# An attention kernel on one Trainium2 core: a new order for the second attention's list, with two scalings moved into it

## The chip, the cores and the metric

The kernel runs on one core of a Trainium2 chip. All data are float32. The metric is the device time of one execution in microseconds; lower is better. The profile uses short names for the engines: PE is TensorE (PEld its weight loads), DVE is VectorE, ACT is ScalarE, POOL is GpSimd, SP is SyncE, which here issues the stores.

## The reference

`x` and `ctx` have 32 batches of 256 tokens with 256 features. The computation, cut to what matters:

```python
# 1. multi-head attention of x over ctx; only batch 0 of its result is used
x = x + attention16(x, ctx, Wq, Wk, Wv)[0]
# 2. first attention of this block, over the layer-normed ctx
nx = layernorm(ctx, norm1_w, norm1_b)
nf = layernorm(x, norm2_w, norm2_b)
att = softmax(nf @ nx.T / 16) @ nx
h = gelu(att @ fc1_w.T + fc1_b)          # 4 hidden units per token
c = h @ fc2_w.T + fc2_b
# 3. second attention: c over itself, after a layernorm
nc = layernorm(c, norm3_w, norm3_b)
s = softmax(nc @ nc.T / 16) @ nc
out = nf + gamma2 * (c + gamma1 * s)
```

The 4 hidden units make everything in part 3 a function of few numbers per token: `c` is 5 numbers (4 and a one) times a fixed matrix, and `nc` is 6 numbers times a fixed matrix. So the kernel computes the second attention on rows of 5 or 6 numbers, and one last product with a fixed matrix `w_out` gives the 256 output features.

## The kernel before, in words

Batches are numbered 0 to 31. Four batches form a group `g` (0 to 7), two form a pair `p` (0 to 15; group `g` holds pairs 2g and 2g+1). All of x stays on the chip in `x_all`, and the output is built up in it.

**First part.** `first_step(s)` for s = 0 to 31 does a step of the first attention for batch s (scores, softmax, transposes), and pieces of layer norms for later batches. `first_step(32)` to `first_step(34)` finish it. In between, steps 20 to 31 already do pieces of the second attention for the first groups.

**norm2_w.** `x_all` holds x normalised but not yet multiplied by norm2_w. `scale_skip(n)` (line 770) does that for batch n: one multiplication on POOL of 128 x 512 numbers by a row that is broadcast. The output of batch n can be added only after it. The list `scaled_at` says at which step of the first part the scalings 0, 1, 2 and so on are issued. Within `first_step` they come after the work that POOL has for later batches.

**The second attention.** It is one list of words, `order`, read from left to right. Each word issues one piece, and each engine does its pieces in the order in which they were issued. The words, for group g or pair p:

- `pre6`, `gelu6`, `m3`, `vg3`, `vgv3`, `var3`, `r3`, `t_k3`: hidden units and layer norm of groups 6 and 7. `n7` copies the last first-attention result to `n_all`. `pre` runs on POOL (lines 993, 995), `gelu` on ACT (996, with a load of its function table), `m` on POOL (1010), `vg` on DVE (1024), `vgv` on POOL (1030), `var` on DVE (1039), `r` on POOL (1046 to 1051, ending in a second product of line 1010, `w_k`), `t_k` on DVE (1055). `t_k2` is the last of these for groups 4 and 5.
- `turn_u g`, `uT g`: four transposes on PE, then a copy out of PSUM (1078). They give the operands of the scores.
- `q p@bank`: first scores of pair p on PE (line 445), `max p` their maxima on DVE (1196), into column NK of `t_sl`.
- `turn_t g`, `tT g`: two transposes and a copy (1088) that bring those maxima into the operand of the second scores.
- `k p@bank`: second scores, less the maxima, and `exp p` on ACT (1209).
- `sums g` (line 357), `col g` (368), `turn_a g` (1117), `a g` (1122, 1123): weighted sums, a copy, transposes, and the division into `v_sl`.
- `turn_v g`, `vT g`: transposes and copy (1088) of `v_sl`.
- `o p@bank`: the output product of pair p on PE, and `add p` on DVE (1214), which adds it to `x_all` and is followed by the store of the two batches from SP's queue (1215, 512 KB).
- `scale n`: `scale_skip(n)` on POOL.

A copy word with `.v` behind it runs on DVE, otherwise on ACT.

**Pair products.** `q`, `k` and `o` are products with 32 rows of weights. Pair p uses partitions 0 to 63 when p is even and 64 to 127 when it is odd. Words joined by `+` are issued interleaved, row group by row group:

```python
for t in range(NC):
    for p, lhs, rhs, dst in pairs:
        for i in range(2):
            r = SL * (p % 2 * 2 + i)
            nc.tensor.matmul(dst[i][:, t, :], lhs[r : r + SL, t * P : (t + 1) * P], rhs[r : r + SL, :], ...)
```

So a product of one pair is 8 matmul records in the profile (float32 gives two each), and of two pairs 16.

**Buffers.** In PSUM, `s0` and `s1` are one buffer of two banks each, `et` has two banks that a pair takes together, and `tp` has two banks that all transposes and `sums` take in turn. A piece waits until the previous user of its banks was read. The copies `ut`, `tt`, `vt` and `col` have three buffers each.

## Time and profile before

| | us |
|---|---|
| median of 3 runs | 230.23 |
| lowest, highest | 229.31, 233.49 |
| profiled execution, own time | 233.63 |
| its span from the first to the last instruction | 231.9 |
| PE busy | 214.7 (93%) |
| POOL busy | 174.8 (75%) |
| DVE busy | 169.8 (73%) |
| ACT busy | 146.8 (63%) |
| mean granted TensorE clock | 0.969 |
| bytes moved | 33.81 MB, 146 GB/s in the mean |

The list takes the last quarter of the span: its first transposes start on PE at 176.59 us, PE's last product starts at 223.09, and the last addition on DVE ends at 227.0. A span row of a window gives busy time, with the number of instructions in brackets, for PE, PEld, DVE, ACT and POOL in that order, and then the granted clock, the share of DMA time and GB/s. Matmuls overlap, so PE's busy time doesn't tell how full it is; the number of instructions in a window helps.

### The profile page before, as it was taken

The numbers are of one execution on the slowest core, as the hardware profiler recorded it, in microseconds if no ns is written. First come the engines' busy times: TensorE is split into PE (matmuls) and PEld (weight loads), VectorE is DVE, ScalarE is ACT, GpSimd is POOL, SyncE is SP. The second block draws the span as 40 slices with busy tenths as digits, with TensorE's granted clock in tenths as the row PEclk, the third lists the DMA queues.
The fourth block names the chain that finished last, engine by engine and source line by source line (L and its number), as shares of the span: only waits on it lengthen the run. The fifth ranks groups of instructions, "written<-read, shape, count | busy, mean of one in ns | idle before, by whom it ended". The sixth has DMA issues, their size and how long they took to land.

```text
span 231.9 us, 4950 instructions
## 1 busy us (share of the span) xinstructions
PE 214.7 (93%) x1797; PEld 155.8 (67%) x1797; DVE 169.8 (73%) x409; ACT 146.8 (63%) x299; POOL 174.8 (75%) x276
## 2 busy tenths in 40 slices
PE   7999898898999989999999999989989999999960
PEld 6766556576787768697897887866665666566540
DVE  1797989899988748667686686766384866588791
ACT  2544978698988285966789967456846753444410
POOL 6057598576989999999979999995189999993000
PEclk9999999999999999999999999999999995699996
DMA  6789997999959964180720000000000130444477
GB/s 212 271 310 371 394 383 148 194 256 236 207 104 335 275 117 170 34 151 2 133 51 1 3 0 0 3 4 4 4 0 3 51 133 0 181 184 181 185 281 264
DMA packets 18038, 33.81 MB, mean 146 GB/s; under 512 B 1175, under 2 KB 2142, under 8 KB 18014
## 3 DMA queue, kind: packets, MB, share of 16 engines
q1 hardware_dynamic: 12974, 24.33, 29.3%
q0 software_dynamic: 3696, 7.34, 18.1%
q10 hardware_dynamic: 1344, 1.84, 2.3%
q8 instruction: 14, 0.23, 0.4%
q14 instruction: 10, 0.08, 0.1%
HBM read 17.73 MB, written 8.39 MB: 113 GB/s over the span
## 4 chain that ended last, share of the span: by engine, by line
PE 53%; POOL 23%; DVE 14%; ACT 5%; issue 2%; DVEq 0%; POOLq 0%; ACTq 0%
PE sc L779 13%; POOL x_all L770 5%; PE k L445 4%; PE pt_x L202 4%; PE o L445 3%; PE pt_c L202 3%; POOL cq L307 3%; DVE st L211 3%; PE pt_e L202 3%; PE pu L357 3%; POOL rs_b L227 3%; PE sc L445 2%; POOL rs_x L227 2%; PE ph L357 2%; PE pf L357 2%
## 5 line engine op out<-in xcount | busy, mean ns | idle before, releaser
L779 PE MATMUL sc<-nxT,nfT 128*128 128x256 f32 x256 | 62.4, 386 | 0.7 <-ACT nfT L761 0.7
L779 PEld LDWEIGHTS sc<-nxT,nfT 128*128 128x128 f32 x256 | 45.7, 190 | 12.1 <-issue 5.3
L770 POOL TENSOR_TENSOR x_all<-x_all,w_bc 128x512 f32<-128x512 f32 x32 | 39.8, 1273 | 0.0
L792 ACT ACTIVATE e<-sc,nm 128x256 f32<-128x256 f32 x64 | 26.9, 473 | 19.0 <-DVE nm L789 18.8
L789 DVE TENSOR_REDUCE nm<-sc 128x2 f32<-128x512 f32 x32 | 22.0, 688 | 22.9 <-PE sc L779 11.1
L761 ACT ACTIVATE nfT<-pt_x,bq,wq 128x256 f32<-128x256 f32 x64 | 33.3, 583 | 1.6 <-PE pt_x L202 1.5
L1214 DVE TENSOR_TENSOR x_all<-o,x_all 128x512 f32<-128x512 f32 (+1 forms) x22 | 19.4, 927 | 8.0 <-PE o L445 8.0
L211 DVE BATCH_NORM_STATS2 st<-x_all 128x6 f32<-128x256 f32 x64 | 23.2, 411 | 0.6 <-DMA x_all<-att 0.5
L1209 ACT ACTIVATE eT<-k 128x1024 f32<-128x1024 f32 (+1 forms) x16 | 14.2, 916 | 13.2 <-PE k L445 10.5
L202 PE MATMUL pt_x<-ident,x_all 128*128 128x128 f32 x132 | 20.8, 280 | 1.5 <-POOL x_all L329 1.3
L202 PE MATMUL pt_c<-ident,cq 128*128 128x128 f32 x132 | 19.7, 276 | 1.5 <-ACT nfT L761 1.0
L202 PE MATMUL pt_e<-ident,e 128*128 128x128 f32 x128 | 19.5, 275 | 1.3 <-ACT eTq L801 0.7
L211 DVE BATCH_NORM_STATS2 st<-cq 128x6 f32<-128x256 f32 x56 | 20.6, 412 | 0.0
L307 POOL TENSOR_SCALAR cq<-cq,rs_b,nmr_b 128x256 f32<-128x256 f32 x32 | 19.4, 680 | 0.0
L202 PEld LDWEIGHTS pt_e<-ident,e 128*128 128x128 f32 x128 | 15.4, 141 | 5.0 <-ACT e L792 1.6
L202 PEld LDWEIGHTS pt_x<-ident,x_all 128*128 128x128 f32 x132 | 15.5, 143 | 4.7 <-POOL x_all L329 2.4
L801 ACT COPY eTq<-pt_e 128x512 f32<-128x512 f32 x32 | 18.4, 588 | 0.3 <-PE pt_e L202 0.3
L345 DVE COPY nxT<-pt_c 128x512 f32<-128x512 f32 x23 | 15.6, 677 | 2.3 <-PE pt_c L202 2.3
L202 PEld LDWEIGHTS pt_c<-ident,cq 128*128 128x128 f32 x132 | 15.0, 141 | 3.1 <-ACT nfT L761 1.9
L331 ACT ACTIVATE x_all<-x_all,nmr_b,rs_b 128x256 f32<-128x256 f32 x16 | 9.8, 618 | 10.9 <-POOL nmr_b L236 10.9
L445 PE MATMUL o<-w_out,vt 32*128 32x256 f32 x128 | 15.0, 448 | 0.6 <-ACT vt L1088 0.5
L445 PE MATMUL k<-tt,ut 32*128 32x256 f32 x112 | 15.3, 441 | 0.1
(222 smaller groups left out, 443.8 us busy)
## 6 DMA issues: line engine op xcount, KB each, us to landing
out_dram<-x_all SPq DMA_DIRECT2D x16, 512.0 KB
x_all<-att POOLq DMA_DIRECT2D x7, 1024.0 KB, 9.3
cq<-in_ctx_dram SPq DMA_DIRECT2D x6, 1024.0 KB
x_all<-in_x_dram SPq DMA_DIRECT2D x4, 1024.0 KB
x_all<-in_x_dram SPq DMA_DIRECT2D x1, 2048.0 KB
x_all<-in_x_dram SPq DMA_DIRECT2D x1, 1792.0 KB
cq<-in_ctx_dram ACTq DMA_DIRECT2D x1, 1024.0 KB
cq<-in_ctx_dram SPq DMA_DIRECT2D x1, 768.0 KB
```

The source lines that it names most:

```text
L202: nc.tensor.transpose(pt[:, dc, t * P : (t + 1) * P], src[:, t, dc * P : (dc + 1) * P], ident)
L211: nc.vector.bn_stats(st[:, t, :], src[:, t, :])
L307: nc.gpsimd.tensor_scalar(row, row, rs[:, i + t, :], nmr[:, i + t, :], ALU.mult, ALU.add)
L357: nc.tensor.matmul(pg[SL * b : SL * (b + 1), 0, :], weights(kc, b), moving[:, b, kc, :], start=(kc == 0), stop=(kc == NC - 1),)
L445: nc.tensor.matmul(dst[i][:, t, :], lhs[r : r + SL, t * P : (t + 1) * P], rhs[r : r + SL, :], start=True, stop=True,)
L761: nc.scalar.activation(nfT_of[n][:, dc, :], px[:, dc, :], AF.Identity, bias=bq[:, dc : dc + 1], scale=wq2[:, dc : dc + 1],)
L770: nc.gpsimd.tensor_mul(x_all[:, n], x_all[:, n], w2_bc.unsqueeze(1).to_broadcast([P, NC, D]))
L779: nc.tensor.matmul(sc[:, qt, :], nfT[:, dc, qt * P : (qt + 1) * P], nxT[:, dc, :], start=(dc == 0), stop=(dc == NC - 1),)
L789: nc.vector.tensor_reduce(nm, sc, AX.X, ALU.max, negate=True)
L792: nc.scalar.activation(e[:, qt, :], sc[:, qt, :], AF.Exp, bias=nm[:, qt : qt + 1])
L801: nc.scalar.copy(eT_of[q][:, b], turned(e_of.pop(n), "et", f"e_{n}"))
L1214: nc.vector.tensor_add(xs, po, xs)
```

## The change

The list is replaced by another order of the same pieces. The pieces keep their engines but for some copies: `vT0`, `vT1`, `vT2`, `uT6`, `tT7`, `col1` and `col4` run on DVE in the new list and on ACT in the old one; `tT4`, `uT5`, `vT3`, `vT4`, `col5` and `col6` the other way round. The products are joined in other pairs and use other banks, group 7 is finished ahead of group 6 (`turn_u7` before `turn_u6`), and `pre6` follows `scale11` where it followed `scale15`. The scalings of batches 10 and 11 are no longer issued in `first_step(32)` but are words of the list.

```diff
-    scaled_at = [25, 26, 26, 27, 27, 28, 29, 29, 31, 31, 32, 32]
+    scaled_at = [25, 26, 26, 27, 27, 28, 29, 29, 31, 31]
...
     order = """
-    turn_v0 scale12 q7@s1+q6@et t_k2 vT0 scale13 turn_t2 max7 sums1 tT2 scale14 max6
-    k5@s0+k4@s1 col1 turn_n7 exp5 scale15 turn_u5 n7 o1@et uT5.v exp4 pre6 turn_t3 add1
-    scale16 q11@s1+o0@s0 tT3 gelu6 sums2 max11 scale17 turn_u4 col2 add0 m3 turn_a1 uT4
-    k7@s1+q10@et scale18 a1 vg3 turn_a2 q8@s0 max10 exp7 vgv3 scale19 turn_v1 var3
-    q9@s1+k6@et a2 vT1 max8 r3 turn_v2 exp6 turn_t5 max9 o2@s0 tT5 vT2 o3@et+k10@s1 add2
-    turn_t4 exp10 add3 sums3 k11@s1+o4@s0 tT4.v col3 scale20 t_k3 turn_a3 exp11 add4
-    turn_u6 scale21 o5@et uT6 a3 scale22 q12@s0+k9@s1 add5 turn_v3 exp9 scale23 max12
-    sums5 k8@s1+q13@et col5.v scale24 vT3.v turn_u7 exp8 max13 scale25 o7@s0 uT7 turn_t6
-    scale26 add7 q15@et+o6@s1 tT6 turn_a5 scale27 max15 sums4 a5 scale28 q14@s0+k13@et
-    col4 add6 turn_a4 exp13 scale29 turn_v5 max14 k12@s1 vT5 a4 scale30 o11@s0+o10@et
-    exp12 turn_t7 add11 scale31 sums6 tT7 add10 k15@s1+k14@s0 col6.v turn_v4 exp15
-    turn_a6 vT4.v a6 exp14 o8@et+o9@s1 sums7 add9 turn_v6 col7 add8 vT6 turn_a7
-    o13@s1+o12@s0 a7 turn_v7 add13 vT7 o14@et add12 o15@s1 add14 add15
+    turn_t2 scale10 q7@s1+q6@et t_k2 tT2 turn_n7 max7 scale11 k5@s0 n7 turn_v0 exp5
+    turn_u4 pre6 vT0.v max6 uT4 scale12 o0@s1+o1@s0 gelu6 turn_t3 add0 sums1 tT3 m3
+    k4@et+q9@s1 col1.v add1 scale13 turn_a1 exp4 turn_u5 max9 scale14 q8@s0 uT5 vg3
+    q11@s1+k6@et a1 vgv3 var3 turn_v1 max8 r3 exp6 sums2 vT1.v k7@s0+q10@et col2 max11
+    turn_a2 exp7 turn_t4 max10 o3@s1 tT4 a2 o2@et+k9@s0 add3 scale15 turn_v2 exp9 sums3
+    vT2.v t_k3 scale16 o5@s0+k8@s1 col3 add2 turn_a3 exp8 scale17 turn_u7 add5 o4@et uT7
+    scale18 a3 q15@s0+q14@s1 add4 scale19 turn_t5 max14 turn_u6 tT5 turn_v3 scale20
+    uT6.v vT3 k10@et+k11@s1 max15 scale21 sums4 exp11 turn_t7 exp10 scale22
+    q12@s1+q13@s0 tT7.v col4.v turn_a4 max12 scale23 sums5 a4 k15@et+o6@s1 col5 scale24
+    max13 turn_a5 exp15 turn_v4 scale25 add6 k14@s0 vT4 a5 scale26 o8@s1+o7@et exp14
+    turn_t6 add8 scale27 sums7 tT6 add7 turn_v5 col7 scale28 o9@s1+k12@s0 vT5 k13@et
+    add9 exp12 scale29 turn_a7 exp13 o10@s0+o11@s1 scale30 a7 sums6 add10 scale31
+    turn_v7 col6 add11 vT7 turn_a6 o15@s0+o14@et a6 turn_v6 add15 vT6 o12@s1 add14
+    o13@s0 add12 add13
     """
```

## The prediction

> **What bounds the kernel now.** First the engines' totals and the clock row of the page.

> ```profile
> PE 214.7 (93%) x1797; PEld 155.8 (67%) x1797; DVE 169.8 (73%) x409; ACT 146.8 (63%) x299; POOL 174.8 (75%) x276
> PEclk9999999999999999999999999999999995699996
> ```

> PE is busy nearly everywhere, and two slices near 200 us show a granted clock far below full. The change touches only what follows 176.59 us, where PE takes up the list. So the second view is that stretch in windows of 3.41 us (columns: busy time and instructions of PE, PEld, DVE, ACT, POOL, then granted clock, DMA share, GB/s).

> ```profile
> 183.57:186.98 3.41, 3.41 (x47) 1.84 (x40) 2.84 (x5) 2.88 (x5) 3.33 (x5) 1.00 0.41 154
> 186.98:190.40 3.42, 3.27 (x22) 1.85 (x26) 2.04 (x6) 1.84 (x3) 3.42 (x5) 1.00 0.42 158
> 190.40:193.81 3.41, 3.41 (x22) 2.22 (x20) 2.45 (x3) 1.84 (x4) 3.33 (x3) 0.50 0.00 0
> 193.81:197.21 3.40, 3.40 (x22) 2.17 (x18) 2.11 (x3) 0.40 (x1) 3.24 (x4) 0.50 0.00 0
> 197.21:200.62 3.41, 3.41 (x30) 1.82 (x32) 1.36 (x3) 1.00 (x2) 3.41 (x4) 0.50 0.82 308
> 200.62:204.03 3.41, 3.41 (x40) 2.25 (x32) 2.65 (x5) 1.61 (x3) 3.41 (x4) 1.00 0.19 73
> ```

> From 190.40 to 200.62 PE runs at half clock. The window ahead of it began only 22 matmuls; the full-clock windows of the list up to 221 otherwise begin 40 or more, and after one with 30 the clock comes back. Why so few? The chain of waits and the timeline say:

> ```profile
> 179.30 4.92 POOL x_all L770 x4
> 184.56 0.29 POOL pre L995
> 184.85 2.46 POOL x_all L770 x2
> 187.31 0.99 POOL w_m L1010
> 188.33 0.57 DVE vg L1024
> 188.90 0.61 DVE t_sl L1196
> 189.55 1.17 PE k L445 x3
> ```
> ```profile
> 188.33 0.57 DVE L1024 TENSOR_REDUCE vg<-w_m 128x80 f32<-128x400 f32 x1 [1.72 <-POOL w_m L1010]
> 188.81 1.28 DVE L1196 TENSOR_REDUCE t_sl<-q 128x2 f32<-128x512 f32 x2
> ```

> POOL works off six scalings (176.79 to 184.2) before `pre6`, so `gelu6` and `m3` come late. DVE stands 1.72 us before `vg3`, with `max10` queued behind it. `max10` must empty the two `et` banks before `k6`, so `q9` runs alone from 188.70 and `k6` from 189.55: two half-filled products after `q8`, itself a single one.

> [...] the trace gives 1.07 us for a product of two pairs (16 matmuls, even and odd pair) and 1.06 for a single one (8). [...]

> **The change part by part.** *PE's work.* Both lists hold 38 pair products in 23 issues, 15 double and 8 single: 15 x 1.07 + 8 x 1.06 = 24.5. Then 7 `sums` x 1.00, 21 turns x 0.37, 4 `turn_u` x 0.59 and `turn_n7` 0.28, in all 41.9, less 0.5 where the last two singles overlap (both lists): 41.4. Nothing is added or removed.

> *What before takes for it.* 176.59 to 224.72 is 48.13. At half clock it did: the rest of `q9`/`k6` 0.75, `turn_v2` and `turn_t5` 0.65, `o2` 1.06, `o3+k10` 1.07, `turn_t4` 0.37, `sums3` 1.00, most of `k11+o4` 0.87 = 5.77 at full-clock prices, in 10.22: 4.45 lost to the clock. That leaves 43.7, so 2.3 are waits: about 1 around `q9`/`k6`, 0.5 before `o14`, the rest small.

> *The scalings.* Two of 1.235 leave POOL's queue after `w_k2` (ends 176.8) and enter the list. POOL then does `scale10`, `scale11` to 179.3, and `turn_n7` has moved up, so `n7` and its reciprocal on DVE end at 179.7 behind `max7`. `pre6` ends at 180.4 (before 184.85), `gelu6` at 182.57 after its 1.28 table load (before 185.15), `m3` 183.6 (188.3), `w_k3` about 192.0 (196.1). Then 17 scalings x 1.235 end at 213.0 (before 12, at 210.90). `add15`, which needs the last two, can start at 216.5, and `add8` needs `scale17`, done 195.7, at 208.3: cost nothing, 3.5 us of cover.

> *The list laid out* by hand at full clock, each engine in its own order, with 0.1 from PE to its reader, max or add 1.14 (1.2 as two halves), exp 0.98 (1.05 as halves), copies 0.34 to 0.6. PE issue, then the last thing that it needs: `k5` 178.31 (`tT2` 177.97); `o0+o1` 180.50 (`exp5` leaves s0 180.45, a wait of 0.17); `k4+q9` 182.94 (`add0` 182.87); `turn_a1` 184.01 (`col1` 183.44); `q8` 184.97 (`add1` 184.58); `q11+k6` 186.03 (`uT5` 185.92); `turn_v1` 187.10 (`a1` 186.6, queued behind `vg3`, whose `m3` is 2 us early); `k7+q10` 188.47 (`exp6` 188.28); `o2+k9` 191.34 (`tT4` 191.03); `o5+k8` 193.78 (`exp9` 193.53); `q15+q14` 196.87 (`uT7` 196.55); `k10+k11` 199.40 (`max14` 199.35, wait 0.13); `q12+q13` 201.84 (`exp11` 201.59); `k15+o6` 204.28 (`max12` 204.2); `k14` 206.09 (`max13` 205.8); `o8+o7` 207.15 (`add6` 206.87); `o9+k12` 209.96 (`add8` 209.5); `k13` 211.03 (`add7` 210.7); `o10+o11` 212.46 (`add9` 212.33); `turn_a6` 215.04 (`col6` 215.0, 0.14); `o15+o14` 215.42 (`vT7`); `o12` 217.38 (`vT6`, 0.52), `o13` to 219.0. Waits about 1.0 where before had 2.3.

> *The end.* After `a6` four adds of two batches remain in both lists, 4.7 us of DVE in one piece: 216.57 to 221.2. Before, its last add ended at 227.0, 222.55 without the 4.45. The last store follows as before: adds every 1.15 us or more, bytes 1.0 us after an add, 1.4 us a store in a row; this puts the last byte 3.2 after the last add (before 230.1 - 227.0 = 3.1).

> *Sum.* The layout gains 222.55 - 221.2 = 1.35. Many margins are under 0.1; bounds on what they give back are 0 and 2.4 (twenty places by 0.12), and I take 0.35. Own time of the profiled execution 233.63 (span 231.9 and 1.7 around it), less 4.45 that the clock took, less 1.0: 228.2. The median of 230.23 and the lowest, 229.31, stand near 233.63 - 4.45 = 229.2, so most runs shown lose little or nothing to the clock, and against them only the 1.0 remains.

> **The rivals.** *Forecast*, 0.53: full clock in the whole list, one microsecond less waiting; 228.2, its own range 227.2 to 229.0. *The wait moves to DVE*, 0.25: DVE has some 17.8 us of work in the layout's 19.4 from `add0` at 181.65 to the end of `max15` at 201.1, and no long pause in it; if a dozen of the thin margins are overrun by 0.1, the gain is gone: 229.4. For it: margins of 0.05 to 0.1 at `o0+o1`, `k4+q9`, `k10+k11`. Against it: between 200.95 and 221.06 before shows PE steps back to back with only 0.4 lost behind such margins. *Slower: the half clock falls into the new list*, 0.17. Its place is between `sums3` and `sums4`, 6.7 us without a `sums`, with `o4` alone among turns: about 32 matmuls in a window, near the 30 at which the clock came back. Three windows cost 4.45: 232.7; one, 1.7: 229.9. It decides from the point where a window begins some 22 to 28, that is where PE stands 0.5 us more there. *More than forecast*, 0.05: the earlier `w_k3` and fewer single products side by side save 1.5 more, 226.7. That the edit does nothing is no rival: POOL's order does change.

> **How the numbers follow.** Likeliest 228.2. From 226.7 to 231.4 I leave out the worst half of the third rival and part of the last. Faster by over 2% means under 225.6, which needs 3.6 us of waits removed where 2.3 exist: 0.05, kept for a comparison with an execution that lost 4.45. Slower by over 2%, above 234.8, needs the half clock and the lost margins together: 0.03. Within 2%, about what a measurement of this kernel can tell from no change: 0.92.

> **What would show it.** Right: `pre6` at about 180, DVE's idle time before `vg3` under 0.3, a granted clock of 1.00 in every window from 176.6, PE's last product near 219, the last add near 221, a span near 226.5. Wrong: PE waiting on `max`, `add` or `exp` in many places of the list by more than 1.5 us in all (rival two); any 0.50 window before 219 (rival three); POOL still scaling when `add15` waits.

## The result, and the profile after

The new list takes 227.96 us in the median of 11 runs (226.96 to 229.17); the kernel before, run beside it, 229.31 in the median of 11. The ratio is 0.9941, with a 95% interval from 0.9922 to 0.9961: the change gains about 1.35 us, 0.6%, which is within 2%. A later comparison, below, gave 0.9912 (0.9892 to 0.9932) for the same kernel, some 2.0 us. Three of those 11 executions of before took some 233.5 us, like the profiled one, in which the clock fell to half within the list; the ratios leave such executions out. The profiled execution of the new kernel took 228.16, its span 226.4. Forecast were 228.2 and "near 226.5".

First the page: PE's busy time and the clock row. PE's 214.7 us have become 208.1 with the same 1797 instructions, and no slice inside the list is under full clock. The 6 at the end is the time after the last product.

```profile
PE 208.1 (92%) x1797; PEld 152.6 (67%) x1797; DVE 169.8 (75%) x406; ACT 146.6 (65%) x301; POOL 175.3 (77%) x276
PEclk9999999999999999999999999999999999999996
```

The same stretch in windows (busy time and instructions of PE, PEld, DVE, ACT, POOL, granted clock, DMA share, GB/s). Before, one such window held 22 matmuls (a count takes in one that runs across the border) and three at half clock, 0.50, followed it. None of these five holds fewer than 38, and DVE is busy for 3.0 to 3.35 of 3.4 us in all five.

```profile
182.60:186.00 3.40, 3.40 (x43) 2.26 (x44) 2.98 (x4) 3.25 (x7) 2.84 (x3) 1.00 0.41 154
186.00:189.40 3.40, 3.40 (x48) 1.96 (x48) 3.25 (x8) 1.60 (x4) 2.62 (x4) 1.00 0.41 154
189.40:192.80 3.40, 3.40 (x45) 2.35 (x38) 3.32 (x6) 1.49 (x4) 3.24 (x4) 1.00 0.02 5
192.80:196.20 3.40, 3.40 (x42) 2.12 (x43) 3.35 (x6) 2.32 (x4) 3.40 (x4) 1.00 0.41 154
196.20:199.60 3.40, 3.32 (x38) 2.31 (x36) 3.19 (x7) 1.21 (x4) 3.40 (x4) 1.00 0.91 343
```

The timeline shows why. On POOL, `pre6` now comes at 180.64 and `m3` at 183.16; they came at 184.56 and 187.31. POOL had to wait 1.00 for `gelu6` and has idle time again. The rest of the scalings is one block of 17 after `w_k3`.

```profile
180.64 0.29 POOL L995 TENSOR_TENSOR pre<-pre,fc1b_all 128x64 f32<-128x64 f32 x1
183.16 1.03 POOL L1010 TENSOR_TENSOR w_m<-v_sl,gram_m 128x400 f32<-128x400 f32 x1 [1.00 <-ACT v_sl L996]
191.47 1.34 POOL L1010 TENSOR_TENSOR w_k<-u_sl,gram_k 128x576 f32<-128x576 f32 x1
192.76 20.98 POOL L770 TENSOR_TENSOR x_all<-x_all,w_bc 128x512 f32<-128x512 f32 x17
```

On DVE, `vg3` follows a maximum without a gap (before: 1.72 us of standing), and the adds of the last four pairs are one piece (five instructions, as one pair is added in halves).

```profile
185.21 1.22 DVE L1196 TENSOR_REDUCE t_sl<-q 128x4 f32<-128x1024 f32 x1
186.34 0.56 DVE L1024 TENSOR_REDUCE vg<-w_m 128x80 f32<-128x400 f32 x1
216.74 4.68 DVE L1214 TENSOR_TENSOR x_all<-o,x_all 128x1024 f32<-128x1024 f32 x5 [0.52 <-PE o L445]
```

PE's timeline names one wait in the whole list, in front of the last two products. It is the 0.52 for `vT6` that the layout gave for `o12`. Shorter stops are not named there: the window from 196.20 above lacks 0.08 us of PE.

```profile
217.52 1.63 PE L445 MATMUL o<-w_out,vt 32*128 32x256 f32 x16 [0.52 <-ACT vt L1088]
```

One difference is not the list's: its first transposes start at 177.02 here and at 176.59 in the profile before, though nothing ahead of them was changed. Over the profiles of all kernels below this start lies between 176.27 and 178.03. So lists are compared by their own length, from that start to the end of the span. Before took 231.9 - 176.59 = 55.31, or 50.86 without the 4.45 that the prediction gives to the half clock. After takes 226.4 - 177.02 = 49.38. The list gained 1.48 us beside the clock; 1.0 was forecast.

### The profile page after: what moved, and what is told of

It is laid out like the page before. It is cut to its first block, busy times and chain, and to the rows that moved or that the text cites. A ratio compares the mean times of both kernels' runs of the same rounds, so it can differ in the third digit from the quotient of the medians.

```text
span 226.4 us, 4951 instructions
## 1 busy us (share of the span) xinstructions
PE 208.1 (92%) x1797; PEld 152.6 (67%) x1797; DVE 169.8 (75%) x406; ACT 146.6 (65%) x301; POOL 175.3 (77%) x276
## 3 DMA queue, kind: packets, MB, share of 16 engines
q10 hardware_dynamic: 1344, 1.84, 2.5%
## 4 chain that ended last, share of the span: by engine, by line
PE 45%; POOL 22%; DVE 14%; DMA 8%; ACT 5%; issue 3%; DVEq 1%; ACTq 0%; SPq 0%; POOLq 0%
PE sc L779 8%; POOL cq L307 6%; PE o L445 4%; DMA x_all<-att 4%; POOL rs_b L227 4%; PE k L445 4%; DVE st L211 4%; PE pu L357 4%; POOL x_all L329 3%; PE sc L445 2%; PE q L445 2%; DVE nm L789 2%; DMA wk_nat<-in_L_xattn_Wk_dram 2%; DMA fc_nat<-in_L_xattn_fc_w_dram 2%; POOL rs_x L227 2%
## 5 line engine op out<-in xcount | busy, mean ns | idle before, releaser
L770 POOL TENSOR_TENSOR x_all<-x_all,w_bc 128x512 f32<-128x512 f32 x32 | 39.8, 1278 | 0.0
L1214 DVE TENSOR_TENSOR x_all<-o,x_all 128x1024 f32<-128x1024 f32 (+1 forms) x20 | 19.3, 1005 | 2.9 <-PE o L445 2.4
L1209 ACT ACTIVATE eT<-k 128x512 f32<-128x512 f32 (+1 forms) x19 | 14.3, 798 | 9.1 <-PE k L445 7.8
L307 POOL TENSOR_SCALAR cq<-cq,rs_b,nmr_b 128x256 f32<-128x256 f32 x32 | 19.4, 679 | 0.0
L445 PE MATMUL o<-w_out,vt 32*128 32x256 f32 x128 | 13.3, 400 | 0.6 <-ACT vt L1088 0.5
L445 PE MATMUL k<-tt,ut 32*128 32x256 f32 x112 | 13.6, 397 | 0.0
```

Of the source, the lines that this page charges most:

```text
L307: nc.gpsimd.tensor_scalar(row, row, rs[:, i + t, :], nmr[:, i + t, :], ALU.mult, ALU.add)
L770: nc.gpsimd.tensor_mul(x_all[:, n], x_all[:, n], w2_bc.unsqueeze(1).to_broadcast([P, NC, D]))
L1214: nc.vector.tensor_add(xs, po, xs)
```

## The experiments

**Theory.** The gain comes from POOL's order alone: with fewer scalings ahead of `pre6` and `m3`, group 6 and 7's layer norm comes in time, DVE's queue doesn't stand and PE's products stay joined. The order of the products themselves matters little. **Rivals:** it comes from the new order of the products; or any edit that takes `vg3` out of `max10`'s way would do; or the list was and is bound by DVE.

### POOL's order alone, in the old list

```diff
-... n7 o1@et uT5.v exp4 pre6 ...             (scale12 to scale15 ahead of pre6, 16 to 19 up to r3)
+... n7 o1@et uT5.v exp4 pre6 scale12 ... m3 scale13 scale14 ... r3 scale15 scale16 scale17 scale18 scale19 ...
```

> The old list with POOL's order of the new one alone: scale12 to scale19 are put behind pre6, m3 and r3, so that pre6 follows scale11. Every other engine keeps the old order. Theory (late POOL work costs before its time): m3 ends near 185.8 instead of 188.3, DVE's idle time before vg3 falls from 1.72 to under 0.3 us, q9 and k6 run as one double product, and 0.8 to 1.0 us go: ratio to before near 0.996, and no window of half clock in the profile. Rival (the order of PE's, DVE's and ACT's pieces makes the gain): under 0.3 us, ratio 0.999 to 1.001.

Measured: 227.88 (22 runs) against 229.33, ratio 0.9951 (0.9936 to 0.9967). That interval overlaps with that of the new kernel (0.9922 to 0.9961), though not with that of its later comparison (0.9892 to 0.9932, on another chip). In the timeline of POOL `m3` comes at 185.69 where it was 187.31, although the list starts 0.85 later here (177.44), and on DVE `vg3` has no idle time ahead of it:

```profile
182.75 0.29 POOL L995 TENSOR_TENSOR pre<-pre,fc1b_all 128x64 f32<-128x64 f32 x1
185.69 1.03 POOL L1010 TENSOR_TENSOR w_m<-v_sl,gram_m 128x400 f32<-128x400 f32 x1 [1.42 <-ACT v_sl L996]
```
```profile
187.37 0.56 DVE L1024 TENSOR_REDUCE vg<-w_m 128x80 f32<-128x400 f32 x1
187.99 1.29 DVE L1196 TENSOR_REDUCE t_sl<-q 128x2 f32<-128x512 f32 x2
```

`q9` and `k6` run joined from 189.64:

```profile
189.64 0.48 PE L445 MATMUL q<-ut 32*128 32x256 f32 x2
189.65 0.48 PE L445 MATMUL k<-tt,ut 32*128 32x256 f32 x2
```

The list has 226.9 - 177.44 = 49.46 us: 1.40 of the 1.48 is had with eight words moved and every product left where it was. By the times the share is smaller: in this same comparison the third experiment below, which has the whole new order, took 227.48 at a ratio of 0.993, so that POOL's order gives 1.1 of 1.6 us by the two ratios. It has between two thirds and nearly all of the gain; that it is the whole of it is not shown. The thinnest window of this list that was read holds 33 matmuls, and its clock is full.

### POOL late again, in the new list

```diff
-... turn_u4 pre6 vT0.v ... (scale12 to scale15 spread behind it)
+... turn_u4 scale12 scale13 scale14 scale15 pre6 vT0.v ...
```

> The new list with scale12 to scale15 put back ahead of pre6, where the old list had them; nothing else. Theory (POOL's lateness is the cost): pre6 ends near 185.3 instead of 180.9, gelu6 holds up tT3 and exp4 on ACT and vg3 holds up a1 and max8 on DVE, PE waits 2 to 3 us more than in the new list: 230 to 231 us, and a window of half clock near 190 in some executions. Rival (margins of the new list absorb it): under 0.5 us more, 228 to 228.5.

Measured: 232.25 (231.46 and 231.48, 233.01 and 233.04), ratio 1.0142 (1.0104 to 1.0179): slower than before, and by more than was expected. The timelines of ACT and PE give the way that it takes. `gelu6` waits for `pre6` with the copies `tT3` and `uT5` queued behind it on ACT, so `turn_a1` and `q11` wait on PE:

```profile
184.87 0.26 ACT L996 ACTIVATE v_sl<-pre 128x64 f32<-128x64 f32 x1 [2.46 <-POOL pre L995]
```
```profile
185.44 0.44 PE L1117 MATMUL pt_a<-ident,col_u 128*128 128x128 f32 x2 [1.09 <-ACT tt L1088]
188.32 0.53 PE L445 MATMUL q<-ut 32*128 32x256 f32 x2 [0.94 <-ACT ut L1078]
190.70 1.71 PE L357 MATMUL pu<-eT,u_sl 128*32 128x256 f32 x16
```

The last of these lines is a `sums`, 1.07 at full clock: the clock fell behind the two waits. The window in which it was low, and the one in front of it (the fall itself lies at 188.63 and the rise at 192.05, and in the 3.41 us up to the fall PE began only 18 matmuls):

```profile
185.60:189.00 3.40, 2.46 (x22) 1.83 (x25) 2.68 (x6) 2.65 (x4) 2.27 (x4) 0.95 0.41 154
189.00:192.40 3.40, 3.40 (x34) 1.32 (x27) 1.56 (x2) 1.08 (x2) 3.24 (x3) 0.55 0.03 5
```

The list has 229.7 - 176.62 = 53.08, 3.70 more than after. Half of the 3.42 us at half clock, an estimate of 1.7 us, was lost to the clock; with the waits of 1.09 + 0.94 that makes 3.73. The two pairs of times here, 1.55 apart, look like one such stretch and two; no profile shows the second. So POOL's order carries the gain in the new list too, and what it guards is worth more than the gain: the new list has less slack against a late `pre6` than the old one, in which the clock fell in only some executions. The profile shows the fall in one of these four executions; for the other three it is read from their times and mean clocks (0.985, 0.973 and 0.973).

### The two scalings back in the first attention's last step

```diff
-    scaled_at = [25, 26, 26, 27, 27, 28, 29, 29, 31, 31]
+    scaled_at = [25, 26, 26, 27, 27, 28, 29, 29, 31, 31, 32, 32]
...
-    turn_t2 scale10 q7@s1+q6@et t_k2 tT2 turn_n7 max7 scale11 k5@s0 ...
+    turn_t2 q7@s1+q6@et t_k2 tT2 turn_n7 max7 k5@s0 ...
```

> The new list with the two scalings of batches 10 and 11 issued in the first attention's last step again, so only this part of the change is undone. POOL does them behind the same w_k2 and ahead of the same pre6 in both: theory expects no difference, 0.998 to 1.002 against the new kernel. Rival (their place counts): slower by 0.5 us or more.

Measured: 227.48 (11 runs), ratio 0.993 (0.9909 to 0.9951), list 225.6 - 176.27 = 49.33. No difference from the new kernel. The scalings of batches 10 and 11 come to POOL behind `w_k2` either way; that they are words of the list now costs and gains nothing.

### The old list with `max10` ahead of `vg3`

Is it enough to take the waiting instruction out of `max10`'s way?

```diff
-... a1 vg3 turn_a2 q8@s0 max10 exp7 ...
+... a1 turn_a2 q8@s0 max10 vg3 exp7 ...
```

> The old list with max10 ahead of vg3 on DVE, everything else as before; POOL stays as late as it was. Theory (k6 waits because max10 is queued behind vg3, which waits for POOL): max10 starts near 187, k6 runs joined with q9 at 188.7, vg3 starts at the same 188.3 as before; 0.7 to 0.9 us gained, ratio near 0.9965, and the half clock gone. Rival (the late w_k3 holds PE up elsewhere, so the wait only moves): under 0.3 us, ratio 0.999 or more.

Measured: 228.83 (14 runs), ratio 0.9988 (0.997 to 1.0006): no gain that can be told from none. `q9` and `k6` were joined, at 188.59, as the prediction's reading of before wants it. But the wait moved on. The timelines of DVE, PE and POOL:

```profile
188.14 0.56 DVE L1024 TENSOR_REDUCE vg<-w_m 128x80 f32<-128x400 f32 x1
189.60 0.24 DVE L1039 TENSOR_REDUCE var<-vgv 128x16 f32<-128x80 f32 x1 [0.90 <-POOL vgv L1030]
```
```profile
190.33 0.41 PE L1063 MATMUL pt_v<-ident,v_sl 128*128 128x128 f32 x2 [0.60 <-DVE v_sl L1123]
191.37 1.13 PE L445 MATMUL o<-w_out,vt 32*128 32x256 f32 x12 [0.41 <-DVE t_sl L1196]
```

```profile
187.99 1.27 POOL L770 TENSOR_TENSOR x_all<-x_all,w_bc 128x512 f32<-128x512 f32 x1
189.22 0.34 POOL L1030 TENSOR_TENSOR vgv<-vg,v_sl 128x80 f32<-128x80 f32 x1
```

DVE now stands at `var3`, for a `vgv3` that POOL begins only at 189.22, behind a scaling. `a2` is queued behind it, `turn_v2` waits for `a2`, and so on. The list has 50.81 us, the 50.86 of before. The separated products were the place where the lateness showed, and not its cause.

### Is DVE the bound?

Two experiments on the new list. One puts ten sums of 128 x 256 numbers, which nothing reads, behind nine maxima and adds and one copy. The other takes three copies from DVE and gives them to ACT.

```diff
+... col1.v wait1 ... max9 wait1 ... add3 wait1 ...     (ten in all)
+        nc.vector.tensor_reduce(idle_dve, w2_bc, AX.X, ALU.add)
```

> The new list with ten extra sums on DVE (128x256 from SBUF, some 0.35 us each, read by nobody) behind col1, max9, max8, max11, max10, add3, add2, add5, add4 and max14: 3.5 us more DVE work between 182.6 and 199.6, where DVE has about 0.9 us idle in the new kernel's trace. Theory (PE and DVE are both nearly full there, so the list stands on thin margins): 2.2 to 2.8 us slower than the new kernel, near 230.3, perhaps with half clock on top. Rival (DVE has room, PE alone sets the pace): under 1 us, 228.5 or less.

Measured: 230.51 (5 runs), ratio 1.0058 (1.0019 to 1.0097). A sum takes 0.41 us in the trace and delays the next instruction by 0.33, so 3.3 were added; the list grew from 49.38 to 229.7 - 178.03 = 51.67, by 2.3. By the ratios it is more, 2.7 us against the new kernel's 0.9941 and 3.3 against its 0.9912. Most of what DVE is given comes out at the end:

```profile
187.40:190.80 3.40, 3.30 (x46) 1.75 (x48) 3.25 (x9) 1.30 (x3) 1.96 (x4) 1.00 0.41 154
190.80:194.20 3.40, 3.35 (x38) 2.21 (x33) 3.37 (x8) 1.45 (x3) 3.24 (x3) 1.00 0.02 5
```

DVE is as busy as in the windows of after, and PE lacks 0.10 and 0.05 us in these two (3.30 and 3.35 of 3.40).

```diff
-... vT1.v ... vT2.v ... uT6.v ...
+... vT1 ... vT2 ... uT6 ...
```

> The new list with the copies vT1, vT2 and uT6 on ACT instead of DVE: 1.28 us less DVE work between 188 and 200, onto an ACT that is idle there by a third or more. Theory (DVE and PE are both full there, so what slows DVE by 3.3 us costs nearly all of it, but PE's own steps stand behind it): at most PE's wait of 0.24 us near 198.7 goes, 0 to 0.3 us gained. Rival (DVE alone sets the pace): 0.8 to 1.2 us gained.

Measured: 228.14 (6 runs), ratio 0.9943 (0.9922 to 0.9964), list 226.1 - 176.59 = 49.51. Nothing is gained. The new kernel itself, beside it, took 227.38, and so did, within 0.01, the kernel below that has the same copies on ACT, so the 0.8 us between them is not put down to the copies. DVE has no room for 3.3 us more, but 1.3 us less on it doesn't shorten anything. What fits is that PE has no gap there that could close: its timeline in this run names only the 0.5 us ahead of `o12`.

### What lets the clock fall

The prediction's third rival put the half clock into the new list, between `sums3` and `sums4`, from about 22 to 28 matmuls in a window. Both experiments lengthen that place, behind `o4`: one with 12 transposes of the identity, the other with 6 products of one row group, two records each. The 1.7 us that the prediction and both expectations give to one window is an estimate: half of 3.41, a third of the 10.24 us at half clock in the kernel before. With POOL late one such stretch came alone, of 3.42 us.

```diff
-... o4@et uT7 ...
+... o4@et fill6 uT7 ...
+        for i in range(12):                               # first experiment
+            nc.tensor.transpose(pf[:, 0, P * (i % 2) : P * (i % 2 + 1)], ident, ident)
+        for i in range(6):                                # second experiment
+            nc.tensor.matmul(pf[:, i % NC, :], ident[0:SL, :], w2_bc[0:SL, :], start=True, stop=True)
```

> The new list with 12 extra transposes of the identity on PE between o4 and q15+q14 (work that nothing reads), so that PE has no wait there but starts few matmuls in a window of 3.4 us: 8 of o4, some 14 transposes, about 24. Theory (the half clock follows a thin window, whether or not PE waits): 2.2 us for the transposes, and in some or all executions one to three windows at 0.50 near 200, another 1.7 to 4.5 us: 232 to 234.5. Rival (the half clock follows PE's waits only): clock 1.00 to the end, 230.2.

> The new list with 6 extra matmuls of 32 rows (one row group of four, 256 columns) on PE between o4 and q15+q14, which nothing reads: 12 records in about 2.6 us at a quarter of the array, without any wait of PE. Theory (the half clock follows how little of the array is used in a window of 3.4 us): clock 0.50 for one to three windows behind it in most executions, 1.7 us or more on top of 2.6 less what was waited there: 231 us or more. Rival (it follows PE's waits): clock 1.00 to the end, 229.5 to 230.

The first measured 228.64 (20 runs), ratio 0.9978 (0.9964 to 0.9993). The transposes took only 1.50 us, 0.12 each, so this tells nothing about a thin window: the thinnest still held 30.

```profile
195.23:198.64 3.41, 3.41 (x30) 2.65 (x32) 2.79 (x6) 1.42 (x2) 3.41 (x3) 1.00 0.74 278
```

The second got its thin window, 23 matmuls, with PE shown busy throughout:

```profile
195.00:198.40 3.40, 3.40 (x23) 2.57 (x24) 2.56 (x5) 1.18 (x2) 3.40 (x4) 1.00 0.79 297
```

Its median was 229.95 (20 runs), ratio 1.0033 (1.0016 to 1.005), about 2 us over the new kernel for the added products. Two of the 20 took 233.36 and 232.94, at a mean clock of 0.975 and 0.974 where the others had 0.986 to 0.992; the profiled one kept the full clock. It had been expected to fall in most executions.

The window above was laid by eye. In the kernel before, the clock is at half for 10.24 us (190.40 to 200.64) and then at full for 27.31, to 227.95, after the last product: three and eight times 3.41. In the new list with POOL late it is at half for 3.42 (188.63 to 192.05), and then at full to about 226.2, by its mean clock of 0.985: one and ten times. That other traces can be counted back in such steps from their last fall is the author's estimate from these two. In this trace that fall lies at about 223.3, by its mean clock of 0.989. So a step would run from about 192.6 to 196.0, and the next to 199.4: the thin stretch lay across a border. Windows near the first place held 48 and 42 matmuls (191.60 to 195.00 and 193.00 to 196.40), and one near the second held 31:

```profile
196.00:199.40 3.40, 3.40 (x31) 2.72 (x29) 1.56 (x4) 0.18 (x1) 3.40 (x3) 1.00 0.95 358
```

The profiles of before and after can be counted so through their lists. In before the clock fell behind 22 matmuls (186.99 to 190.40) and behind 2 at the end, stayed at half behind 22 and 22, came back behind 33, and stayed full behind 35 and more. In after it stayed full behind 30 and more, and fell at the end behind a window with none. With POOL late it fell behind 18. In the windows laid by eye, 28 kept the clock in the old list with `max10` first (189.40 to 192.80), and so did the 23 above. PE's busy time does not part them: the clock fell behind 3.26 us of it in the kernel before and stayed full behind 2.53 at the end of the new list (216.11 to 219.52). It counts matmuls that overlap once: the 128 of `o` in before took 448 ns each in the mean and 15.0 us together. Nor does a count alone, for other shapes: in the first part of the kernel before, a window with 14 matmuls (81.18 to 84.59) keeps the full clock. And the steps, counted back from the last fall, lie elsewhere in each profile: in three of the new order (the new kernel, the same again, the two scalings back) one begins about 1.5, 1.9 and 2.7 us behind the list's start. If the clock does go by such windows, a thin stretch hardly longer than one of them would cost it in some executions only. That is the author's reading; that it parted the 2 from the 18 is not shown, as the two have no profile.

In the kernel before, 12 of the 106 executions of these comparisons show the half clock by their times. The old list with POOL early and the new list, whose windows ahead of the last products held 32 or more where they were read, showed none in 22 and 28 executions; nor did, in 14, the old list with `max10` first, though a window of it held 28 matmuls and lacked 1.1 us of PE. At a rate of 12 in 106, 14 executions without any would still come about one time in five.

```profile
189.40:192.80 3.40, 2.30 (x28) 1.36 (x24) 3.06 (x6) 1.73 (x4) 3.32 (x4) 1.00 0.02 5
```

### The end of the list

The prediction puts the last byte 3.2 us behind the last add. Three kernels, all from the new list: the last add of two batches split into two of one batch, each with its own store; the same for the last four pairs; and this together with the three copies on ACT. The new kernel itself ran once more beside the second and third; the first ran earlier, on another chip.

```diff
     def output(p, pieces):
+        if p == 15:                                       # p >= 12 in the second
+            for i in range(2):
+                n = 2 * p + i
+                nc.vector.tensor_add(x_all[:, n], pieces[0][2][:, i], x_all[:, n])
+                nc.sync.dma_start(by_tokens(out[n : n + 1]), x_all[:, n : n + 1])
+            return
```

> The new list with add15 done as two additions of 128x512, each with a store of its own (256 KB). The last four stores follow add15 without a pause in the new kernel's trace (bytes from 219.05 to 224.5, idle 0.5 us before). Theory (the end is set by the stores' bytes behind the first of the last four adds): bytes start some 0.57 us earlier, the end moves by 0.4 to 0.55 us, ratio to before 0.001 to 0.002 below the new kernel's. Rival (the last addition sets the end): no gain, and 0.06 us lost for the second addition.

> The new list with the adds of pairs 15, 14, 12 and 13 all done by batch, each with its own store of 256 KB. With pair 15 alone split, the stores' bytes paused again at 219.7 for want of add14. Theory (the end is set by bytes that wait for adds): no pause after add15's first half, the last byte comes 2.4 to 2.6 us after the last add instead of 3.05; 0.3 to 0.5 us gained against the new kernel, less 0.15 for the second additions. Rival (the last addition and its fixed delay set the end): no gain, or 0.1 to 0.2 us lost.

> Both: the three copies on ACT and the last four pairs stored by batch. If the two act on different stretches their gains add: 0.4 to 0.7 us below the new kernel, near 227.0 or ratio 0.991 to before. If either has no effect, the other's gain alone remains.

> The new kernel itself on the same chip, as the measure for the three others: ratio 0.993 to 0.995 to before, and no execution with half clock in the list.

| kernel | median us (6 runs each) | ratio | list us |
|---|---|---|---|
| last add split | 227.28 | 0.9927 (0.99 to 0.9954) | 225.5 - 176.36 = 49.14 |
| last four split | 227.32 | 0.9918 (0.9892 to 0.9944) | 225.9 - 176.91 = 48.99 |
| both edits | 227.39 | 0.9914 (0.9891 to 0.9937) | 225.7 - 176.59 = 49.11 |
| new kernel again | 227.38 | 0.9912 (0.9892 to 0.9932) | 225.7 - 176.43 = 49.27 |

In the traces the split does what it is meant to. Windows of 1 us, of after and then of the kernel with the last four split (the last two columns are DMA share and GB/s): after has a hole between stores at 218, the split kernel none, and there the bytes end 2.4 us after the last add (221.51), in after about 3.05 (221.42, to the middle of the window from 224).

```profile
218.00:219.00 1.00, 1.00 (x15) 0.70 (x12) 1.00 (x2) 0.00 (x0) 0.00 (x0) 1.00 0.55 205
224.00:225.00 1.00, 0.00 (x0) 0.00 (x0) 0.00 (x0) 0.00 (x0) 0.00 (x0) 0.50 0.54 199
```
```profile
218.00:219.00 1.00, 1.00 (x14) 0.80 (x10) 1.00 (x2) 0.00 (x0) 0.00 (x0) 1.00 1.02 379
223.00:224.00 1.00, 0.00 (x0) 0.00 (x0) 0.00 (x0) 0.00 (x0) 0.00 (x0) 0.50 0.86 330
```

The last add itself comes 0.2 us later in its list. That leaves 0.3 to 0.4 us of list, and the times don't show it: all four ratios lie within 0.0015 of one another. The new kernel's own was put at 0.993 to 0.995 and came out at 0.9912 where it had been 0.9941, so two comparisons of one kernel can lie 0.003 apart. No version here is faster than the new kernel by anything that was measured.

## Why the prediction was right, and where it was not

- **The bound of the list.** Right. `pre6` was put at 180.4 and `m3` at 183.6; with the later start of 0.43 they would end at 180.8 and 184.0, and ended at 180.93 and 184.19. The 17 scalings were to end at 213.0 + 0.4, and ended at 213.74, 3.0 us ahead of the last adds. The experiment with POOL's order alone shows that this is the main cause of the gain: 1.40 of 1.48 by the lists, about two thirds by the ratios. What is left goes to the new order of the products and copies, as far as these comparisons can tell it from none.
- **The mechanism at `max10`.** Half of it. That `vg3` stood on DVE with `max10` behind it and that this separated `q9` from `k6` is in the trace. But the experiment with `max10` first shows that this step alone was worth nothing; `vgv3`, `var3` and `a2` were late for the same reason and took over. The prediction laid out what comes next only with POOL early, where the question does not arise.
- **The 4.45 of the clock.** Full clock in every window of the list, as forecast, in the profile; and no time of the new kernel among 11 and then 6 that would need a half clock.
- **The layout.** Its 42.41 us from PE's start to the end of the last product (219.0 - 176.59) were 42.13 (219.15 - 177.02), and its 44.61 to the last add were 44.40. The one wait that the profile names, 0.52 ahead of `o12`, was in it to the hundredth.
- **The step that failed: the 0.35 given back for thin margins.** Nothing was given back: the list was 0.2 better than laid out, so the gain was 1.48 where 1.35 - 0.35 = 1.0 was put down. The forecast of 228.2 for the profiled execution came out as 228.16 because the first part happened to take 0.43 longer than in the profile before; two errors of half a microsecond cancelled. Against the runs beside it, whose ratio means 1.35 us, the forecast was 0.35 short; against the later comparison, 1.0.
- **"The wait moves to DVE".** It did not come about, though its premise holds: DVE is full to 3.0 to 3.35 of 3.4 us, and 3.3 us more on it cost 2.3 or more. A chain at the edge need not be over it.
- **The half clock in the new list.** It did not come about; the place that was named, from 195.8 to 199.2, held 34 matmuls where the rival reckoned with 32 and needed 22 to 28. The rival's count was of the right size: counted in steps of 3.41 us, the clock fell behind 22 matmuls in the list of before and 18 with POOL late, and stayed full behind 30 and more in after. What lies between was not met in such steps, and what makes the clock fall is not shown: a window with 14 products of other shapes kept it. Why the kernel before lost it in 12 of 106 executions only is not shown either.

What stays open besides is the start of the list, which moves by over 1 us between executions of the same first part.

## What to carry to other kernels

Work that fills an idle engine (here the scalings on POOL) should be queued behind the short steps of any chain that others wait for, up to its own due time; moving eight such words gave two thirds or more of what a wholly new order gave. When a stall is removed at the place where it shows, look at the next instruction that needs the same late engine before counting the gain. And compare a stage by its own length: the part ahead of it can vary by as much as the gain (here the list began between 176.27 and 178.03).
